# A sequence's mean row put into all rows by one matmul, in a cross-attention and quantised feed-forward kernel

## The chip, the cores and the metric

The kernel runs on one core of one Trainium2 chip. The metric is the device time of one execution in microseconds (us). Each time is the median of the runs named beside it.

## The reference

The reference does one layer on x of shape (4, 2048, 512): four sequences of 2048 rows. First comes cross-attention to a context of 154 rows for each sequence, with 16 heads of 64, and then a feed-forward part with quantised weights.

```
mask = j_idx % n_q == i_idx              # n_q = 2048 rows, n_kv = 154 keys
sim  = where(mask, q @ k^T * scale, -max)
out  = softmax(sim) @ v                  # then @ Wout + bout
x    = x + attention(layernorm(x), context)

h    = layernorm(layernorm(x)) * gamma + beta
h    = qlinear(h, w1, b1)                # rows rounded to 127 steps, w to -1, 0, 1
h    = gelu(h)
x    = x + qlinear(h, w2, b2)
```

The mask leaves query i only key i where i is below 154. For every later row the whole line of scores has one value, so the softmax is even and the row gets the mean of all 154 values. With W = Wv Wout, what attention adds is `context[i] @ W + bout` for rows 0 to 153, and `mean(context) @ W + bout` for rows 154 to 2047. Queries and keys need no arithmetic.

## The kernel before

A tile is 128 rows. There are 64 tiles, 16 for each sequence, and in each sequence the order is tiles 2 to 15, then 0 and 1. So tiles 0 to 13 in the order of work are rows of the first sequence that need only the mean row; tiles 14 and 15 need the 128 first rows ("front") and a mixed tile of 26 keyed rows and 102 mean rows ("second").

Each engine has one queue, in which it works in order. The order of all instructions is written out by hand as strings of words: BEGINNING (line 83) for the start up to tile 11, STEADY (line 118) for four tiles at a time, and ENDING (line 127). A word is a letter code with numbers, and the table `words` maps it to a function. Words of different engines in one string are put into different queues. The words that matter here:

- `lv`, `lo`: load pieces 0 to 7 of Wv and Wout; `w`: four float32 matmuls that add one piece's product into W (line 415); `cw`: copy a quarter of W from PSUM into w_sb (lines 426, 428), on DVE with a last figure of 1 and on ACT with 0.
- `lc`: load the context; `sk`: sum of the keys (line 431); `mk`: mean into row 32b of ctx_rest (434); `lk`: keys 128 to 153 into the rows behind it (437). ctx_rest holds, for each of the four sequences, the mean and the 26 last keys in 32 rows.
- `pr0.2`, `pr2.4`: the product of ctx_rest with W, in two halves of two matmuls (line 444); `yr`: bout added, into y_rest (454); `sr`: y_rest stored to DRAM (481), from which `s` and `t` spread rows of it into `second` and `mean` tiles for the sequences.
- `Yb.0.2`, `Yb.2.4`, `y`: the front rows of sequence b, in two halves (444), and bout added (489).
- `lw`, `ms`, `z`, `q`, `c`: load a chunk of w1 (first figure 0) or w2 (1), sum its absolute values, form the scale of all, round, clip to -1..1. `z` puts a sum of all partitions through PE (`z.1`, "pt", line 206). A last figure of 1 is DVE; with 0 it is ACT for `ms` and `q`, and POOL for `c`.
- `L`: load two tiles of x; `a` (POOL) or `A` (DVE): add the attention row to tile n (246); `S`: row statistics (253); `O`, `o`, `C` or `N`: the scale of the double layer norm for a group of tiles, by DVE with one step on POOL, or all on POOL (269 to 276); `P`, `E` (DVE), or `k` (POOL) or `n` (ACT) with `e` (POOL, lines 311 and 312): normalise and apply gamma and beta; `R`: the largest value of a row (334); `V` (POOL) or `v` (DVE): the group's scales (348, 350); `Q`: round to the 16-bit form (354); `T`: transpose by DMA (365).
- `U`: the up product, 16 matmuls (534); `I`: seed of a half of its PSUM tile with the bias, on ACT or DVE (526, 524); `G`: gelu of a half (553); `M`: its largest value (565); `H`: round (594); `h`: transpose by DMA (605); `W`: the down product, 16 matmuls (612); `D`: its scale (587); `X`, `x`: b2 added (328); `F`, `f`: finish (618) and store.

Groups of tiles for the scales are of sizes 1, 1, 1, 1, 2, 2, 2, 3, 3, and then 4. Group 8 is thus tiles 13 to 15, and `V13` forms the scales of that group. PSUM tiles: three of 1024 columns for `U` (pool ps_h), and two of 512 columns (ps_o), which `pr`, the mean, `z`, `Y` and `W` share. Twelve buffers of one ring hold x pairs and weight chunks; a load waits until a buffer's earlier content has been used.

The mean row of the first sequence is needed first of all. Before, it has a product of its own: `sf` spreads the key sum over 128 columns (line 461), so that `pm` (four matmuls, line 444) writes the mean row of the product into all 128 rows of PSUM. `m` (661) adds bout on DVE and keeps it in SBUF for POOL's additions. For tile 0 `xo` adds bout to x early (476), and `A0` adds the bare product from PSUM.

Of the kernel before, what the change touches and what calls it, by code (L numbers as in the profile page):

```python
# [37 lines left out]
F32 = mybir.dt.float32  # L38
# [3 lines left out]
ALU = mybir.AluOpType  # L42
# [3 lines left out]
P = 128  # L46
# [7 lines left out]
def xattn_ffn(ctx: ExitStack, tc, x, ctxT, WvT, Wout, bout, w1T, b1, w2T, b2, gamma, beta, out):  # L54
    nc = tc.nc
    B, S, D = x.shape
    NKV = ctxT.shape[1] // B
    INNER = Wout.shape[0]
    HID = w1T.shape[1]
    KD, KI, KH = D // P, INNER // P, HID // P  # L60
# [16 lines left out]
    for g, size in enumerate(sizes):  # L77
# [40 lines left out]
    STEADY = """
        U0 G0.0 I1.0.1 M0.0 W-2 G0.1 I1.1.0 M0.1 Q2 F-2 L14 f-2 D-1
# [42 lines left out]
    ones = constant([P, P], F32, "ones")  # L162
# [15 lines left out]
    def x_of(n):  # L178
        return pairs[n // 2][:, n % 2, :]
# [217 lines left out]
    sums = constant([P, KD, B], F32, "sums")  # L397
# [6 lines left out]
    for half in range(2):  # L404
# [4 lines left out]
            start=True,  # L409
            stop=True,  # L410
# [31 lines left out]
    def rows(lhs, dst, ks=range(KD)):  # L442
        for k in ks:
            nc.tensor.matmul(dst, lhs(k), w_sb[k], start=(k == 0), stop=(k == KD - 1))
# [13 lines left out]
    def spread_keys():  # L460
# [170 lines left out]
    def by_half(f):  # L631
# [29 lines left out]
        "m": lambda: nc.vector.tensor_tensor(mean[0], py["mean"], bout_b, ALU.add),  # L661
# [93 lines left out]
```

## Time and profile before

| | |
|---|---|
| median of 3 runs | 524.63 us (524.53 to 524.99) |
| the profiled execution's own time | 525.17 us |
| its span | 523.2 us |
| busy: PE, DVE, ACT, POOL | 501.1, 433.2, 426.3, 410.5 us |
| granted TensorE clock, mean | 0.99 |
| moved by DMA | 94.00 MB, 180 GB/s on average |

The span goes from the first to the last instruction; the execution's own time has 1.97 us around it. Times in the views are microseconds from the start of the span. PE is the matmuls (TensorE), DVE VectorE, ACT ScalarE, POOL GpSimd, SP the engine that issues all DMAs. A line of a timeline gives start, duration, engine, source line, operation, output and inputs, their sizes, the number of instructions merged, and in brackets the idle time before and what ended it. A float32 matmul is two entries there. The granted clock is a share of full speed.

### The profile page before, as it was taken

The page shows a single profiled execution, that of the slowest core. Times are in us where ns is not written, and L with a number is a line of the kernel's source. Part 1 is how long each engine was busy: PE and PEld are TensorE (multiplying, and loading weights), DVE is VectorE, ACT ScalarE, POOL GpSimd, SP SyncE. Part 2 cuts the span into 40 slices and gives each one's busy share as a digit, 9 for nine tenths or more (in the row PEclk, how much of TensorE's full clock was granted, in tenths as well). Part 3 has the DMA queues.
Part 4 walks back from the last instruction along what each step waited for, and adds up shares of the span by engine and source line. Part 5 has one row for each costly group of instructions (what it writes and reads, how often), then busy time and mean ns, then how long its engine had stood idle before and what let it go on. Part 6 is the DMA issues. An engine that isn't in the chain of part 4 may idle for free.

```text
span 523.2 us, 6893 instructions
## 1 busy us (share of the span) xinstructions
PE 501.1 (96%) x2168; PEld 223.8 (43%) x2168; DVE 433.2 (83%) x753; ACT 426.3 (81%) x393; POOL 410.5 (78%) x532
## 2 busy tenths in 40 slices
PE   8997987999999989999999989999999899999996
PEld 3443432444444434444444434444444344444442
DVE  0188999889799889899999988999999888787762
ACT  2278987999788879888888878888889798888971
POOL 0048999999999999899999898999999998852220
PEclk9997998999999999999999999999999999999999
DMA  8998569376979695858697987679586956575664
GB/s 289 399 391 306 188 132 200 84 178 137 195 161 221 141 199 139 201 137 201 149 205 160 178 183 180 164 164 198 133 203 128 201 112 147 110 166 132 135 112 125
DMA packets 194112, 94.00 MB, mean 180 GB/s; under 512 B 170268, under 2 KB 170268, under 8 KB 194076
## 3 DMA queue, kind: packets, MB, share of 16 engines
q1 hardware_dynamic: 194076, 93.56, 75.1%
q8 instruction: 17, 0.28, 0.2%
q14 instruction: 19, 0.16, 0.1%
HBM read 34.55 MB, written 17.04 MB: 99 GB/s over the span
## 4 chain that ended last, share of the span: by engine, by line
PE 57%; POOL 18%; DMA 10%; DVE 6%; ACT 4%; issue 3%; SPq 1%; DVEq 0%; ACTq 0%; POOLq 0%
PE ph L534 27%; PE po L612 26%; DMA xqT<-xqg 6%; PE wps L415 4%; POOL x L246 4%; POOL h L312 3%; POOL h L311 3%; DVE m L565 2%; POOL x L328 2%; DMA x<-x_dram 2%; ACT hq L594 2%; DMA wv<-WvT_dram 2%; POOL h L306 1%; POOL r L270 1%; ACT hid L553 1%
## 5 line engine op out<-in xcount | busy, mean ns | idle before, releaser
L534 PE MATMUL ph<-w1q,xqT 128*128 128x512 f16 x1024 | 233.4, 381 | 10.1 <-DMA xqT<-xqg 7.8
L612 PE MATMUL po<-w2q,hqT 128*128 128x512 f16 x1024 | 231.3, 379 | 1.9 <-DMA hqT<-hq 1.2
L565 DVE TENSOR_REDUCE m<-hid 128x1 f32<-128x1024 f32 (+1 forms) x130 | 153.1, 1192 | 27.0 <-ACT hid L553 26.6
L553 ACT ACTIVATE hid<-ph,d 128x1024 f32<-128x1024 f32 (+1 forms) x130 | 140.9, 1095 | 31.4 <-PE ph L534 30.1
L534 PEld LDWEIGHTS <-xqT 128*128 128x128 f16 x1024 | 100.0, 98 | 135.2 <-DMA xqT<-xqg 12.1
L612 PEld LDWEIGHTS <-hqT 128*128 128x128 f16 x1024 | 100.0, 98 | 123.4 <-DMA hqT<-hq 2.2
L594 ACT ACTIVATE hq<-hid,i 128x2048 f16<-128x2048 f32 (+1 forms) x65 | 128.2, 1974 | 28.3 <-ACT ph L526 10.2
L526 ACT ACTIVATE ph<-b_b,inv 128x1024 f32<-128x1024 f32 x86 | 95.3, 1112 | 3.2 <-POOL inv L348 2.1
L312 POOL TENSOR_TENSOR h<-h,beta_b 128x512 f32<-128x512 f32 x59 | 75.6, 1282 | 4.6
L311 POOL TENSOR_TENSOR h<-h,gamma_b 128x512 f32<-128x512 f32 x59 | 75.0, 1271 | 3.9
L328 POOL TENSOR_TENSOR x<-x,b_b 128x512 f32<-128x512 f32 x61 | 77.0, 1272 | 0.0
L246 POOL TENSOR_TENSOR x<-x,mean 128x512 f32<-128x512 f32 x52 | 65.7, 1273 | 5.0 <-DVE mean L661 3.8
L618 DVE SCALAR_TENSOR_TENSOR o<-po,d,x 128x512 f32<-128x512 f32 x64 | 47.8, 746 | 16.0 <-PE po L612 10.6
L524 DVE TENSOR_SCALAR ph<-b_b,inv 128x1024 f32<-128x1024 f32 x42 | 53.2, 1267 | 0.6 <-ACT hid L553 0.6
L334 DVE TENSOR_REDUCE m<-h 128x1 f32<-128x512 f32 x64 | 42.9, 673 | 5.0 <-POOL h L312 5.0
L354 ACT ACTIVATE xqg<-h,s 128x512 f16<-128x512 f32 x64 | 45.4, 712 | 1.6 <-DVE s L342 1.6
L587 POOL TENSOR_TENSOR d<-mh,wm 128x1 f32<-128x1 f32 x64 | 12.5, 206 | 41.2 <-DVE mh L580 37.4
L253 DVE BATCH_NORM_STATS2 bn<-x 128x6 f32<-128x512 f32 x64 | 43.4, 679 | 0.6 <-POOL x L246 0.6
L306 POOL TENSOR_SCALAR h<-x,rstd,shift 128x512 f32<-128x512 f32 x54 | 41.9, 776 | 0.2
L415 PE MATMUL wps<-wo,wv 128*128 128x512 f32 x64 | 28.1, 595 | 1.5 <-DMA wv<-WvT_dram 1.5
L222 POOL TENSOR_SCALAR w1q<-wi 128x1024 f16<-128x1024 int16 x6 | 6.3, 1070 | 27.7 <-DVE wi L217 27.5
L415 PEld LDWEIGHTS wps<-wo,wv 128*128 128x128 f32 x64 | 11.9, 190 | 17.3 <-issue 13.9
(76 smaller groups left out, 261.3 us busy)
## 6 DMA issues: line engine op xcount, KB each, us to landing
x<-x_dram SPq DMA_DIRECT2D x32, 512.0 KB, 4.2
out_dram<-o SPq DMA_DIRECT2D x64, 256.0 KB, 2.8
ws<-w1T_dram SPq DMA_DIRECT2D x8, 512.0 KB, 7.2
ws<-w2T_dram SPq DMA_DIRECT2D x8, 512.0 KB, 9.6
wv<-WvT_dram SPq DMA_DIRECT2D x8, 256.0 KB, 8.5
wo<-Wout_dram SPq DMA_DIRECT2D x8, 256.0 KB, 4.5
ctx_sb<-ctxT_dram SPq DMA_DIRECT2D x1, 1232.0 KB
hqT<-hq SPq DMA_TRANSPOSE x65, 4.3
```

The costliest lines, as they stand in the source:

```text
L246: e.tensor_tensor(x_of(n), x_of(n), y, ALU.add)
L311: nc.gpsimd.tensor_tensor(normed[n], normed[n], gamma_b, ALU.mult)
L312: nc.gpsimd.tensor_tensor(normed[n], normed[n], beta_b, ALU.add)
L328: e.tensor_tensor(x_of(n), x_of(n), b2_b, ALU.add)
L415: nc.tensor.matmul(wps[k // 2][:, (k % 2) * 512 : (k % 2 + 1) * 512], wv[c][:, k * P : (k + 1) * P], wo[c], start=(c == 0), stop=(c == KI ...
L524: nc.vector.tensor_scalar(ph, row, d, None, ALU.mult)
L526: nc.scalar.activation(ph, row, AF.Identity, bias=0.0, scale=d)
L534: nc.tensor.matmul(bank[i], xqT[n][:, k, :], w1q[:, k, i * 512 : (i + 1) * 512], start=False, stop=(k == KD - 1), skip_group_check=True,)
L553: nc.scalar.activation(hidden[n][:, i * w : (i + 1) * w], up_ps[n][half][:, lo : lo + w], AF.Gelu, bias=0.0, scale=deq1[g][:, j : j + 1],)
L565: nc.vector.tensor_reduce(m2[:, i : i + 1], hidden[n][:, i * w : (i + 1) * w], AX.X, ALU.max, apply_absolute_value=True,)
L594: nc.scalar.activation(hq[n][:, lo : lo + w], hidden[n][:, lo : lo + w], AF.Identity, bias=0.0, scale=inv2[n],)
L612: nc.tensor.matmul(po, hqT[n][:, k, :], w2q[:, k, :], start=(k == 0), stop=(k == KH - 1))
```

## The change

The mean is no longer a product of its own. Row 0 of y_rest, which is the first sequence's mean row with bout already added, is multiplied by a row of 128 ones: one float32 matmul with a single row on both sides (`pm`), which puts it into all 128 rows of PSUM. `A0` adds that to tile 0, with no `xo` before it. `m0` copies it to SBUF on ACT. So `sf`, `xo` and three matmuls are gone, and both halves of `pr` and `yr` now stand before the mean.

BEGINNING is laid out anew, with nearly the same words in another order: other orders of the loads, seven of eight w1 chunks measured on DVE (three before), one w2 chunk measured on DVE, `lr2` (beta) before five w2 loads, `Y1` and `Y2` before `Y0` and `Y3`, `sr` before U0, and the work of some tiles moved between engines: three more `k` and one more `a` on POOL, one `V` fewer there, three `n` fewer on ACT, and single `c` and `X` words exchanged between POOL and DVE. STEADY and ENDING stay.

```
     BEGINNING = """
...
-        w7 lw1.3 ms1.4.0 sk0 c0.4.0 lw1.7 c0.7.0 cw0.1 q0.1.0 sf c0.0.0 cw1.0 lw1.1 pm0.2
-        lr2 cw3.1 cw2.0 lk q0.3.0 c0.1.1 mk pm2.4 xo1 ms1.6.0 L2 q0.6.1 c0.6.1 L3 ms1.2.0
-        Y0.0.2 m lb0 A0 a1 ms1.5.0 S0 Y0.2.4 ms1.0.0 O0 P0 o0 a2 ms1.3.0 C0 pr0.2 S1
-        ms1.7.0 a3 O1 y0 ms1.1.0 c0.3.0 S2 o1 E0 a5 z1.0 R0 z1.1 z1.2 Q0 O2 Y3.0.2 P1 o2
-        q1.6.0 T0 a6 C2 q1.2.0 L4 C1 lb1 V0 lr3 q1.0.0 E1 c1.2.0 Y3.2.4 R1 I0.0.0 P2 V1
-        q1.3.0 pr2.4 a4 y3 S3 Q1 a8 I0.1.0 T1
-        U0 O3 S4 L5 L6 c1.6.0 q1.7.0 S5 o3 E2 end G0.0 c1.0.0 C3 I1.0.0 R2 a7 I1.1.0
...
+        lo0 lv0 lv1 lv2 lw0.5 lo1 lv3 lo2 lv4 w0 lw0.0 lw0.2 lo3 lw0.4 lw0.1 w1 lw0.6 lo4
...
+        sk1 w7 L1 c0.2.0 q0.1.0 sk2 c0.0.0 mk lw1.2 lk cw0.0 cw1.0 c0.6.1 lw1.1 q0.7.0
+        pr0.2 cw3.1 cw2.1 ms1.0.0 c0.7.0 L2 lb0 ms1.6.1 pr2.4 q0.3.0 ms1.3.0 c0.3.0 L3 yr
+        lr3 c0.1.0 pm Y1.0.2 A0 m0 S0 ms1.4.0 a1 O0 P0 ms1.5.0 o0 a2 S1 ms1.2.0 C0 a3
+        ms1.7.0 S2 O1 ms1.1.0 E0 o1 a4 R0 O2 Q0 V0 z1.0 S4 z1.1 a5 I0.0.0 T0 z1.2 lb1 C1
+        sr Y2.0.2 q1.4.0 a6 S5 q1.5.0 L4 o2 P1 N4 q1.1.0 L5 P2 E1 I0.1.0
+        U0 L6 c1.4.1 R1 a7 q1.0.0 C2 Q1 a8 S3 q1.2.0 T1 Y2.2.4 V1 O3 A9 o3 I1.0.0 k5 S6
+        end G0.0 c1.0.0 S7 I1.1.0
+        U1 c1.5.0 y2 C3 k4 G0.1 N6 E2 q1.6.0 P3 Y1.2.4 E3 G1.0 R2 c1.2.0 q1.7.0 Y0.0.2 k7
+        M0.0 Q2 V2 c1.1.0 y1 q1.3.0 T2 Y0.2.4 R3 e4 G1.1 v3 Y3.0.2 M0.1 Q3 I2.0.0 T3 X1 L7
+        t1 I2.1.0 M1.0
+        U2 k6 H0 e5 S8 M1.1 I3.0.0 h0 Y3.2.4 e6 S9 G2.0 R4 G2.1 R5 N8 I3.1.0
+        U3 c1.7.1 A10 Q4 c1.6.1 H1 c1.3.1 T4 D0 y0 L8 V4 M2.0 a13 W0 I4.0.0 h1 y3 X0 L9
+        M2.1 Q5 e7 G3.0 T5 s0 L10 I4.1.0
...
+        U5 a12 G4.1 R8 D1 S13 a11 Q6 M4.1 H3 T6 k9 t2 W2 V6 f0 e9 S11 I6.0.0 h3 F1 G5.0
...
+        U11 T12 M10.0 I12.0.0 M10.1 k16 G11.0 k17 D8 W9 R15 e16 H10 F8 M11.0 G11.1 h10 e17
+        S22 I12.1.0 M11.1 n18 Q13 a23 T13 R16 H11 f8 D10 F9 V13 e18 R17 f9 h11 X11 X10
...
-    first_mean = att.tile([P, KD, P], F32, tag="first_mean", name="first_mean")
-    def spread_keys():
-        nc.vector.tensor_scalar(
-            first_mean, sums[:, :, 0:1].to_broadcast([P, KD, P]), 1.0 / NKV, None, ALU.mult,
-        )
-    def mean_rows(lo, hi):
-        if lo == 0:
-            py["mean"] = ps_o.tile([P, 512], F32, tag="po", name="py_mean")
-        rows(lambda k: first_mean[:, k, :], py["mean"], range(lo, hi))
-    def add_bout(vector):
-        e = nc.vector if vector else nc.gpsimd
-        e.tensor_tensor(x_of(0), x_of(0), bout_b, ALU.add)
+    def mean_rows():
+        py["mean"] = ps_o.tile([P, 512], F32, tag="po", name="py_mean")
+        nc.tensor.matmul(py["mean"], ones[0:1, :], y_rest[0:1, :], start=True, stop=True)
+    def keep_mean(vector):
+        if vector:
+            nc.vector.tensor_copy(mean[0], py["mean"])
+        else:
+            nc.scalar.copy(mean[0], py["mean"])
...
-        "m": lambda: nc.vector.tensor_tensor(mean[0], py["mean"], bout_b, ALU.add),
-        "sf": spread_keys,
-        "xo": add_bout,
+        "m": keep_mean,
```

## The prediction

> **What bounds the kernel now.** I read first how busy each engine is, over the span and by stage.
>
> ```profile
> PE 501.1 (96%) x2168; PEld 223.8 (43%) x2168; DVE 433.2 (83%) x753; ACT 426.3 (81%) x393; POOL 410.5 (78%) x532
> ```
>
> The same by stages:
>
> ```profile
> 40.00:50.00 10.00, 6.32 (x12) 2.76 (x11) 7.91 (x26) 7.50 (x12) 8.71 (x11) 0.75 0.83 301
> 50.00:60.00 10.00, 9.47 (x32) 3.87 (x31) 8.91 (x22) 8.88 (x10) 9.54 (x13) 0.91 0.76 249
> 60.00:70.00 10.00, 10.00 (x36) 4.53 (x35) 9.72 (x19) 9.17 (x11) 9.32 (x16) 1.00 0.33 93
> 70.00:80.00 10.00, 7.47 (x31) 2.97 (x29) 9.76 (x18) 8.70 (x9) 9.26 (x16) 1.00 0.84 192
> 80.00:90.00 10.00, 6.94 (x24) 2.56 (x23) 9.72 (x18) 7.45 (x8) 9.52 (x11) 0.83 1.05 194
> 200.00:480.00 280.00, 276.60 (x1280) 124.90 (x1279) 252.49 (x422) 241.43 (x211) 246.55 (x302) 1.00 0.75 163
> ```
>
> The columns after a stage's length are the busy time of PE, its weight loads, DVE, ACT and POOL, then the granted clock. From 200 to 480 us PE idles 3.4 us of 280: PE sets the pace there. Between 40 and 90 it does not: PE has holes and loses clock, and POOL and DVE are the full ones.
>
> The timeline of PE shows where the holes end (idle in brackets):
>
> ```profile
> 33.76 3.60 PE L444 MATMUL py_mean<-w_sb,first_mean 128*128 128x512 f32 x8
> ...
> 40.62 1.88 PE L444 MATMUL py_rest<-w_sb,ctx_rest 128*128 128x512 f32 x4
> 45.67 0.59 PE L206 MATMUL pt<-tot,ones 128*128 128x1 f32 x2 [3.17 <-DVE tot L203]
> 46.77 6.23 PE L444 MATMUL py<-w_sb,ctx_sb 128*128 128x512 f32 x8 [0.50 <-DVE wm L209]
> ...
> 85.72 5.31 PE L534 MATMUL ph<-w1q,xqT 128*128 128x512 f16 x16 [2.39 <-DMA xqT<-xqg]
> ...
> 190.10 3.63 PE L534 MATMUL ph<-w1q,xqT 128*128 128x512 f16 x16 [2.06 <-DMA xqT<-xqg]
> ```
>
> The line at 85.72 is U4. After it PE runs without a hole until 190.1. So any time won before U4 counts in full only if the other engines can feed U5 to U19 earlier as well. POOL's timeline answers that:
>
> ```profile
> 38.16 1.27 POOL L246 TENSOR_TENSOR x<-x,mean 128x512 f32<-128x512 f32 x1 [3.76 <-DVE mean L661]
> 46.19 1.27 POOL L246 TENSOR_TENSOR x<-x,mean 128x512 f32<-128x512 f32 x1 [1.29 <-DMA x<-x_dram]
> ...
> 150.36 0.19 POOL L348 TENSOR_TENSOR inv<-s,sw 128x3 f32<-128x3 f32 x1
> ```
>
> From a1 (38.16) to V13 (150.36), POOL's gaps over 0.13 us are three: 0.52, 1.29 and 0.29, 2.1 us in 112. POOL is a second bound, running beside PE, from the moment the mean exists. V13 gives the scale of the seed I13.0, which U13 needs, and the margin is small: DVE starts I13.0 at 151.04 (it was waiting for e17 by way of R17; V13's result was there 0.4 us before), ends it at 152.3, and PE takes U13 at 153.03. So U13 could have come 0.7 + 0.4 = 1.1 us earlier as far as V13 goes.
>
> **The change part by part.**
>
> *PE work removed.* A float32 matmul of 512 columns is two passes here: py_mean's four take 3.60 us, 0.9 each. Four go (3.6), one comes. It has one row of weights and data; no row of the trace has such a shape. Below: nothing; above: the two passes of a full one, by py_rest (four passes 1.88, start to start 0.43, the last 0.59), 0.43 + 0.59 = 1.02. The Trainium skill, "TensorE: Matmul & The Clock Gate", section "Why this matters for your kernels", speaks against a cheap row: a single matmul of few rows takes as long as one of 128. By its rule the mean comes 1.0 us after y_rest, in proportion to the rows at once; I take 1.0. Net on PE: 3.6 - 0.9 = 2.7 us less.
>
> *When the mean exists.* Loads: until lo1, 1.83 MB are asked for; before, the third w1 piece, with as much before it, was read at 9.30. So w1 waits about 1.45 us, as w2 did before (1.47), and the 32 products end at 33.9 again. The other seven pieces of Wout and Wv fall in before need at the 0.398 MB/us that the landings at 12.83 (3.15 MB) and 29.15 (9.65 MB) give. DVE: sk, mk, lk are over at about 32.8; cw3, cw2 follow the products, 33.95 to 35.3, inside pr. Then pr, four matmuls, 33.9 to 37.5; yr on DVE 0.68, to 38.2; pm 38.3 to 39.3; ACT copies the mean (by the w_sb copies, 0.59) to 39.95. So a1 starts at 40.0, not 38.16: **1.85 us later**, in spite of less PE work, because y_rest and a trip DVE to PE to ACT lie in the chain. A0 reads PSUM at 39.35, before at 38.00.
>
> *Removed from DVE:* sf 0.67, xo 0.68 and m 0.69, 2.0 us, before A0. DVE gets four more chunks of w1 to measure (seven for three, 1.22 each), at 14 to 26 us under the loads: tot comes at 26.6 after 25.3, and pt sits between w5 and w6, where PE is until 26.9, so nothing is lost; uncovered it would be 1.3 us. ACT sheds as many.
>
> *Until U0.* beta landed at 44.80 and held E0 for 0.73. It is now ordered before five chunks of w2 and lands near 36.5. But the mean is later and tot now stands before S4 on DVE; S1, C0, S2, O1, E0, R0 run from 41.75 to 46.2. ACT has seven measures queued before Q0, the last landing at 44.6, so Q0 starts at 47.0 (46.69 before). T0 goes at 47.65 (47.44). PE has nothing between Y1.0.2 (42.1) and pt (47.2): a hole of 5 us where it was 3.17.
>
> *The clock.* The same page, section "What's actually happening", puts the fall to half clock after an idle window of about 3.4 us. By that rule the old hole (3.17) would cost nothing and the new one would. The rows differ: after 3.17 the clock was 0.50 and Y3 took 6.23, not 3.6; after 2.39, U4 took 5.31, not 3.6; after 2.06 nothing was lost. I go by the rows: both holes cost, so the new one costs no more than the old: Y2.0.2, started at 48.5 behind wm, takes four slow passes, 4.9 us, and U0 starts at 53.4 (54.55 before). By the rule it would be 2.6 us worse against before.
>
> *U0 to U4.* R1 is at 53.85 (51.67) because c1.4, P2, E1 and two stats stand before it, so T1 lands near 60 and U1 is late (58.70 before). Then PE runs U1, Y1.2.4, Y0, Y3.0.2, U2, Y3.2.4, U3, W0: 4 x 3.45 + 10 x 0.9 = 22.8 from 60.3, to 83.1. T4: e5 on POOL ends near 75 to 76, R5, Q4, T4 sent at 78, landed (3.8 by the old one) at 82. U4 at 83.1 with no hole: 2.6 us earlier, and without the 1.7 of lost clock, 4.3 in all.
>
> *SP.* y_rest's store sr now stands before L4, and t1, which reads it back, before h0 (issues of 0.34 and 0.56 by the old rows). The rows are ready by then, and h0 goes out near 72 with W0 due at 79.7, so this is hidden; uncovered it would be 0.9 at W0.
>
> *U5 to U13: what is kept.* POOL's work from a1 to V13, by kind, after minus before: a +1 (1.24), k +3 (0.8 each, 2.4), d +1 (0.15), X -1, c -2 (1.02 each), inv/d pair -1 (0.3): +0.2. Its start +1.85. Its waits: only L2's landing at 46.15 is seen, 0.85 in place of 2.1: -1.25. V13 is thus +0.8 if POOL's slow instructions recur (c at 1.56 and 1.43, h at 1.60 twice against 1.02 and 1.27: about 2 us before V13), and -1.2 if none does. I take the middle, -0.2 to 0, call it **0**. Then U13 comes 1.1 us earlier, not 4.3: PE gives back about 3 in small waits at U6 (V6 at 96 to 97.5 sets I6.0; 94.7 before), at W4 (h4 behind H4 on ACT) and at U13. Behind V13, X11 and X10 move ahead of N20: +1.07 for group 10, for which R19 leads to H14 and I16; U16 had 2.1 us of room, so 1.0 stays. From there on PE has the same work.
>
> *Sum.* Profiled execution: span 523.2, its own time 525.17 (1.97 around it). 523.2 - 1.1 = 522.1, or 524.07 with what lies around; the median of the runs is 0.54 under the profiled one: **523.5**.
>
> **Rivals.**
>
> *The lead survives.* If POOL meets no slow instruction and V13 is over 1 us early, and ACT keeps up, the 4.3 at U4 stay but for small change: 524.6 - 4 = 520.6. For it: U4 was the last hole for 100 us. Against: ACT's and POOL's rows of 80 to 150 are full too.
>
> *Nothing is left.* V13 at +1 and the rooms at U13 and U16 used up: 524.6. For it: the sum of POOL's work is not smaller, and the mean is later.
>
> *Slower, by the clock.* PE reaches U13 4 us ahead, V13 comes at +1 or later, and the hole before U13 passes the length at which the clock falls (between 2.06 and 2.39 by the rows). U13 then takes 5.3, not 3.6: +1.7, with 0.1 from V13: 526.4. For it: two such holes already cost 2.6 and 1.7. Against: waits at U6 and W4 share the lead out in pieces under 2 us.
>
> **How the numbers follow.** My own chain 0.40 (523.5, alone 522.6 to 524.4), the lead survives 0.22, nothing left 0.15, slower by the clock 0.23. 0.2% is 1.05 us, about what a measurement of this kernel can tell from no change. Faster: 0.28 of my chain and 0.22; same: 0.12 and 0.14; slower: 0.23 and 0.01. The range goes from the first rival with one more us (519.5) to the last with 0.4 more (526.8).
>
> **What would show it.** The mean copied near 39.9 and a1 at 40; one py_mean matmul of two passes; U0 near 53.4 behind a slow Y2; U1 near 60; U4 near 83 at full clock; V13 within 1.2 us of 150.4; PE waits at U6 and U13 for seeds. It is wrong if U0 or U1 come much earlier, if POOL's V13 is before 148.5, or if a stall of transposes or a slow U13 shows after 140.

## The result, and the profile after

| | before | after |
|---|---|---|
| median | 524.58 us | 528.38 us (527.17 to 528.67) |
| profiled execution's own time | 525.17 us | 528.67 us |
| its span | 523.2 us | 526.9 us |
| ratio after / before | | 1.0065, 95% interval 1.0049 to 1.0081 |

The changed kernel is slower by 3.8 us between the medians, 3.4 by the ratio, where 1.1 us less was forecast. Measured again in a later batch, the ratio was 1.0067 (1.0050 to 1.0083). First the busy line of the page, of the kernel after:

```profile
PE 499.8 (95%) x2162; PEld 222.1 (42%) x2162; DVE 433.6 (82%) x754; ACT 421.1 (80%) x383; POOL 413.6 (79%) x534
```

PE's work went down and the span went up, so the time is in waits. The stages of the kernel after (columns as in the table of before: length, busy PE, weight loads, DVE, ACT, POOL, then clock, DMA share, GB/s):

```profile
40.00:50.00 10.00, 3.13 (x7) 1.53 (x6) 8.78 (x26) 8.82 (x15) 9.32 (x10) 0.80 0.85 306
50.00:60.00 10.00, 8.04 (x23) 2.68 (x21) 7.14 (x20) 6.17 (x7) 7.21 (x15) 0.86 0.88 248
60.00:70.00 10.00, 8.77 (x29) 4.04 (x30) 9.72 (x19) 8.91 (x10) 9.34 (x18) 1.00 0.08 15
80.00:90.00 10.00, 8.69 (x41) 3.75 (x40) 9.13 (x16) 7.94 (x8) 9.26 (x17) 1.00 0.81 190
200.00:480.00 280.00, 277.46 (x1285) 125.22 (x1284) 253.49 (x424) 242.20 (x212) 247.37 (x304) 1.00 0.75 163
```

Between 50 and 60 POOL is busy for 7.21 of 10 us (8.71 to 9.54 in all stages of before that were shown). That is new. Its timeline, kernel after, names its wait for the mean and the one wait over 0.13 us between a1 and V13 (idle in brackets):

```profile
40.68 1.26 POOL L244 TENSOR_TENSOR x<-x,mean 128x512 f32<-128x512 f32 x1 [2.13 <-ACT mean L463]
...
57.76 1.75 POOL L244 TENSOR_TENSOR x<-x,mean 128x512 f32<-128x512 f32 x1 [2.12 <-DMA x<-x_dram]
...
153.35 0.20 POOL L346 TENSOR_TENSOR inv<-s,sw 128x3 f32<-128x3 f32 x1
```

V13 ends up 3.0 us later than before. PE's timeline, kernel after, shows where that arrives:

```profile
38.13 1.12 PE L457 MATMUL py_mean<-y_rest,ones 1*128 1x512 f32 x2 [0.78 <-DVE y_rest L452]
...
47.21 0.59 PE L204 MATMUL pt<-tot,ones 128*128 128x1 f32 x2 [6.05 <-DVE tot L201]
48.62 3.78 PE L442 MATMUL py<-w_sb,ctx_sb 128*128 128x512 f32 x4 [0.82 <-DVE wm L207]
...
61.23 3.70 PE L521 MATMUL ph<-w1q,xqT 128*128 128x512 f16 x16 [2.78 <-DMA xqT<-xqg]
...
82.80 3.61 PE L599 MATMUL po<-w2q,hqT 128*128 128x512 f16 x16 [1.31 <-DVE front L476]
...
155.02 3.62 PE L521 MATMUL ph<-w1q,xqT 128*128 128x512 f16 x16 [0.57 <-DVE ph L511]
...
193.01 5.20 PE L521 MATMUL ph<-w1q,xqT 128*128 128x512 f16 x16 [2.32 <-DMA xqT<-xqg]
```

U13 starts at 155.02 instead of 153.03 (+2.0). U18 starts at 193.01 instead of 190.10 (+2.9) and takes 5.20 us (3.63 before), because the granted clock is 0.51 in its first 3.3 us. PE is then 4.5 behind. Of this 0.8 comes back at the three later waits for transposes and the last one (0.66, 0.57, 1.30, 0.32 after; 0.45, 1.33, 1.62, 0.29 before), which leaves the 3.7 by which the spans differ.

The way from POOL to U18 is read off DVE's and SP's timelines of the kernel after:

```profile
180.14 0.69 DVE L332 TENSOR_REDUCE m<-h 128x1 f32<-128x512 f32 x1 [0.90 <-POOL h L310]
...
186.27 0.75 DVE L605 SCALAR_TENSOR_TENSOR o<-po,d,x 128x512 f32<-128x512 f32 x1
```

```profile
187.05 0.36 SPq L610 DMA_DIRECT2D out_dram<-o  x1
187.51 1.23 SPq L363 DMA_TRANSPOSE xqT<-xqg  x1
```

and the same three places of the kernel before:

```profile
176.10 0.69 DVE L334 TENSOR_REDUCE m<-h 128x1 f32<-128x512 f32 x1 [0.91 <-POOL h L312]
...
182.23 0.75 DVE L618 SCALAR_TENSOR_TENSOR o<-po,d,x 128x512 f32<-128x512 f32 x1
```

```profile
183.01 0.36 SPq L623 DMA_DIRECT2D out_dram<-o  x1
183.48 1.70 SPq L365 DMA_TRANSPOSE xqT<-xqg  x1
```

R20 on DVE waits for e20 on POOL (the number behind a letter is the tile); behind R20, in DVE's order, stand I17.0, M16 and F14; the store f14 waits for F14; T18 stands behind f14 on SP. From R20's start to T18's issue it is 7.37 us after and 7.38 before. The whole 4.0 us that e20 is late reach T18. From T18's issue to U18 it was 5.50 us after and 6.62 before, so that 2.9 of the 4.0 reach U18. Before, R20 waited for POOL too, with the same 0.9 us: POOL's lag did set T18 already, and the forecast looked for it only as far as V13.

The chain that the profile follows back from the last instruction, to what released each step, runs the same way. Pieces of it in the kernel after (start, length, what):

```profile
50.87 0.51 SPq L468
...
51.47 6.13 DMA x<-x_dram
...
57.76 1.75 POOL x L244
...
178.84 1.28 POOL h L310
...
187.51 5.45 DMA xqT<-xqg
```

It goes over the store `sr` (line 468) and L4 to POOL, and stays on POOL from 57.76 to 180.12, but for 1.2 us on DVE. In the kernel before it is on POOL from 106.1 to 176.08 and goes on to T18 in the same way: POOL was on the chain there too.

### The profile page after: what moved, and what is told of

The parts are those of the page before. It is cut to its first block, busy times and chain, and to the rows that moved or that the text cites. A ratio compares the mean times of both kernels' runs of the same rounds, so it can differ in the third digit from the quotient of the medians.

```text
span 526.9 us, 6889 instructions
## 1 busy us (share of the span) xinstructions
PE 499.8 (95%) x2162; PEld 222.1 (42%) x2162; DVE 433.6 (82%) x754; ACT 421.1 (80%) x383; POOL 413.6 (79%) x534
## 4 chain that ended last, share of the span: by engine, by line
PE 56%; POOL 23%; DMA 8%; DVE 7%; issue 3%; ACT 2%; SPq 0%; POOLq 0%; DVEq 0%; ACTq 0%
PE ph L521 26%; PE po L599 25%; DMA xqT<-xqg 5%; POOL x L244 5%; PE wps L413 5%; POOL h L310 4%; POOL h L309 4%; POOL x L326 3%; POOL h L304 2%; DVE m L552 2%; ACT hq L581 1%; DMA wo<-Wout_dram 1%; DMA x<-x_dram 1%; POOL r L268 1%; DVE bn L251 1%
## 5 line engine op out<-in xcount | busy, mean ns | idle before, releaser
L513 ACT ACTIVATE ph<-b_b,inv 128x1024 f32<-128x1024 f32 x87 | 96.4, 1111 | 6.8 <-POOL inv L346 4.9
L244 POOL TENSOR_TENSOR x<-x,mean 128x512 f32<-128x512 f32 x53 | 67.5, 1280 | 4.3 <-ACT mean L463 2.1
L511 DVE TENSOR_SCALAR ph<-b_b,inv 128x1024 f32<-128x1024 f32 x41 | 51.9, 1266 | 0.4 <-POOL inv L346 0.4
L304 POOL TENSOR_SCALAR h<-x,rstd,shift 128x512 f32<-128x512 f32 x57 | 44.4, 779 | 0.2
L220 POOL TENSOR_SCALAR w1q<-wi 128x1024 f16<-128x1024 int16 x7 | 7.6, 1098 | 29.6 <-DVE wi L215 26.8
L226 DVE TENSOR_REDUCE part<-ws 128x1 f32<-128x1024 f32 x8 | 9.4, 1213 | 17.9 <-DMA ws<-w1T_dram 17.9
```

Of the source, the lines that this page charges most:

```text
L244: e.tensor_tensor(x_of(n), x_of(n), y, ALU.add)
L304: nc.gpsimd.tensor_scalar(h, x_of(n), rstd[g][:, j : j + 1], shift[g][:, j : j + 1], ALU.mult, ALU.add)
L513: nc.scalar.activation(ph, row, AF.Identity, bias=0.0, scale=d)
```

## The experiments

Theory A: POOL's wait for L4, carried by V13 to U13, and further to U18's clock. B: PE's own holes in the front. C: the mean's lateness as such. D: POOL's load and lateness up to V13, of which A and C are parts. E: ACT is as full as POOL, so that work moved to it gains nothing. F, formed last: the time goes by POOL's lag at e20, which sets T18; V13 is only a part of it. A diff is against the changed kernel unless it names another base. Each ratio is to before as measured beside the run on the same chip; e1 to e4, e5 to e8, e9 to e11, e12, e13 to e16, and e17 with e18 were measured together. The expectations call the tiles 9, 12, 13, 14, 15 and 17 of the moved normalisations groups. The landmarks of all runs, each from its own profiled execution:

| run | a1 | V13 | U13 | T18 issued | U18 | ratio to before (95%) |
|---|---|---|---|---|---|---|
| before | 38.16 | 150.36 | 153.03 | 183.48 | 190.10 | 1 |
| changed | 40.68 | 153.35 | 155.02 | 187.51 | 193.01 | 1.0065 (1.0049 to 1.0081) |
| e1 L4 early | 40.93 | 151.50 | 153.15 | 185.68 | 190.20 | 1.0048 (1.0034 to 1.0063) |
| e2 old mean, new layout | 39.04 | 151.19 | 152.86 | 185.41 | 191.24 | 1.0041 (1.0016 to 1.0066) |
| e3 new mean, old layout | 40.23 | 151.46 | 153.56 | 184.58 | 190.18 | 0.9995 (0.9981 to 1.0008) |
| e4 hole of U18 filled | 41.29 | 152.32 | 153.98 | 186.48 | 191.65 | 1.0055 (1.0036 to 1.0075) |
| e5 POOL less | 41.12 | 150.93 | 153.96 | 185.05 | 189.99 | 1.0015 (0.9998 to 1.0033) |
| e6 POOL less, L4 early | 41.28 | 149.53 | 152.84 | 183.68 | 189.83 | 0.9983 (0.9970 to 0.9997) |
| e7 old layout, POOL less | 39.77 | 150.50 | 153.69 | 184.41 | 190.13 | 0.9955 (0.9937 to 0.9974) |
| e8 before, POOL less | 37.60 | 150.08 | 152.47 | 183.17 | 188.26 | 0.9970 (0.9957 to 0.9983) |
| e9 before, POOL more | 38.74 | 153.13 | 155.24 | 186.19 | 191.53 | 1.0032 (1.0021 to 1.0043) |
| e10 as e7, three moved | 39.41 | 149.47 | 153.88 | 183.08 | 188.71 | 0.9959 (0.9947 to 0.9971) |
| e11 as e6, copy first | 39.71 | 149.03 | 152.05 | 183.19 | 188.51 | 0.9978 (0.9968 to 0.9988) |
| e12 as e11, a fourth moved | 40.60 | 150.06 | 153.09 | 184.20 | 189.96 | 0.9992 (0.9981 to 1.0004) |
| e13 L4 early, copy first | 40.13 | 152.01 | 153.68 | 186.24 | 191.28 | 1.0029 (1.0012 to 1.0045) |
| e14 changed, again | 40.59 | 153.76 | 155.42 | 187.91 | 192.83 | 1.0067 (1.0050 to 1.0083) |
| e15 L4 early, again | 40.86 | 151.68 | 153.34 | 185.86 | 190.90 | 1.0029 (1.0012 to 1.0045) |
| e16 new mean, old layout, again | 40.25 | 151.39 | 153.50 | 184.49 | 190.33 | 1.0003 (0.9991 to 1.0015) |
| e17 L4 early, X10 on DVE | 40.44 | 151.44 | 153.10 | 184.38 | 189.31 | 1.0008 (0.9996 to 1.0021) |
| e18 L4 early, X10 ahead of V13 | 40.82 | 152.46 | 154.11 | 185.38 | 190.20 | 1.0026 (1.0015 to 1.0038) |

**L4 early (e1).** Of SP's words around T0 in the kernel after, with the new store of y_rest (line 468) between bias and L4 (line 174, three loads merged):

```profile
49.33 0.56 SPq L385 DMA_DIRECT2D b_b<-b_dram  x1
49.98 1.40 SPq L468 DMA_DIRECT2D rest_dram<-y_rest  x1
51.47 1.60 SPq L174 DMA_DIRECT2D x<-x_dram  x3
```

```
-        sr Y2.0.2 q1.4.0 a6 S5 q1.5.0 L4 o2 P1 N4 q1.1.0 L5 P2 E1 I0.1.0
-        U0 L6 c1.4.1 R1 ...
+        Y2.0.2 q1.4.0 L4 a6 S5 q1.5.0 o2 P1 N4 q1.1.0 L5 P2 E1 I0.1.0
+        U0 L6 sr c1.4.1 R1 ...
```

> The changed kernel with one move on SP's queue: the load L4 is issued ahead of the store of y_rest (sr), which goes behind L6; every other queue keeps its order. Theory A (POOL): POOL's wait of 2.1 us for L4 before a8 (55.64 to 57.76) is carried on to V13, V13 holds U13, and what is lost there lengthens the hole before U18 beyond the length at which the clock falls. Then L4 lands near 56, V13 comes near 151.5 instead of 153.35, U13 near 153.3 instead of 155.02, U18 runs at full clock, and the time is 3 to 3.5 us under the changed kernel's: 525. Theory B (PE): the loss is PE's own, from the hole of 6 us before pt, the slow Y2 and the late U1; none of these is touched, so 528.4 stays, within 0.7.

The wait of 2.12 is gone and V13 is 1.85 earlier, as theory A has it. The time follows less: 1.0048 here and 1.0029 when run again (e15), against 1.0065 and 1.0067, so 0.9 to 2.0 us of the 3.4 to 3.5. A is a part.

**Old mean in the new layout (e2).** `sf`, `pm` in four matmuls, `xo` and the addition of bout are put back; `pr` and `yr` come behind the mean, and `ms1.6.1` goes one line down.

```
-        pr0.2 cw3.1 cw2.1 ms1.0.0 c0.7.0 L2 lb0 ms1.6.1 pr2.4 q0.3.0 ms1.3.0 c0.3.0 L3 yr
-        lr3 c0.1.0 pm Y1.0.2 A0 m0 S0 ...
+        pm0.2 cw3.1 cw2.1 ms1.0.0 c0.7.0 L2 lb0 xo1 pm2.4 q0.3.0 ms1.3.0 c0.3.0 L3
+        lr3 c0.1.0 Y1.0.2 m A0 pr0.2 pr2.4 S0 ...
```

> The changed kernel's layout with the mean as it was before: spread keys, four matmuls, bout added on DVE; y_rest's product follows behind it on PE, in the hole before pt. Theory A (POOL): a1 starts near 38.2 again, but a8 still cannot start before L4 has landed at 57.7, so POOL's wait there grows from 2.1 to over 4 us and V13 stays within 0.5 us of 153.35; the time stays at 528, within 0.8. Theory C (the mean's own lateness): the 2.5 us by which a1 is late are what is lost, so the time falls by 2 to 3.5 us, to 525 to 526.5. Theory B (PE): the hole before pt is partly filled, the four matmuls come back (2.7 us of PE work): between 1 us under and 2.7 us over the changed kernel.

a1 is 1.6 us earlier and V13 2.2, yet the ratio stays at 1.0041: the new layout costs with the old mean as well. So C is a part at most. Theory A had POOL's wait for L4 grow here; in the trace it is gone, because `sr`, at the same place ahead of L4, took SP only 0.38 us. So e2 is a second run without that wait, and stands where e1 does.

**New mean in the old layout (e3).** The BEGINNING of before, with the mean made as in the change.

```
 (base: before)
-        q0.1.0 sf c0.0.0 cw1.0 lw1.1 pm0.2
-        lr2 cw3.1 cw2.0 lk q0.3.0 c0.1.1 mk pm2.4 xo1 ms1.6.0 L2 q0.6.1 c0.6.1 L3 ms1.2.0
-        Y0.0.2 m lb0 A0 a1 ...
+        q0.1.0 mk lk c0.0.0 cw1.0 lw1.1 pr0.2
+        lr2 cw3.1 cw2.0 q0.3.0 c0.1.1 pr2.4 ms1.6.0 L2 q0.6.1 c0.6.1 L3 yr ms1.2.0
+        pm Y0.0.2 A0 m0 lb0 a1 ...
```

> The old layout with the new mean only: sf, xo and the four matmuls out; both halves of pr, yr, pm, A0 and the copy on ACT in their place. All else as before. Theory A (POOL): a1 starts near 40.5, 2.4 us later than 38.16, but POOL's waits of 0.5, 1.3 and 0.3 us behind it take up most of that; V13 comes 0.4 to 1.0 later, inside the 1.1 us of room at U13; 524.6, within 0.8. Theory C (the mean's own lateness): 2 to 3 us over before: 527. If the 2.7 us of PE work taken out count: 522.

No difference: 0.9995, and 1.0003 when run again (e16). a1 is 2.1 late, V13 only 1.1, because L2's landing, for which POOL had waited 1.29, now comes first. The new mean costs nothing where such a wait takes its lateness up. What costs is the layout.

**The hole of U18 filled (e4).** Ten extra matmuls run ahead of U18, into the PSUM tile that W16 overwrites; nothing else changes.

```
+            if word == "U2" and n == 16:
+                fill(16, 10)
```

> The changed kernel with ten matmuls more, of 512 columns (2.2 us), in the hole of 2.32 us that PE has before U18; their product goes into the PSUM tile of W16 and is overwritten. Theory of the clock: the hole of 2.32 us is what halves the clock for U18 (5.20 us instead of 3.6). Filled, U18 takes 3.6 and the time falls by 1.6 us to 526.8, although PE has more to do. If the clock falls for another reason, or the loss is made good later, 528.4 stays.

PE's timeline of this kernel shows them, and U18 at full clock:

```profile
189.49 2.32 PE L599 MATMUL po<-w1q,xqT 128*128 128x512 f16 x10
191.65 3.62 PE L521 MATMUL ph<-w1q,xqT 128*128 128x512 f16 x16
```

The ratio is 1.0055. By the difference of the two ratios the clock at U18 is 0.5 us of the 3.4, and the intervals overlap. In the second trace of the changed kernel (e14) U18 kept its clock (3.63 us after a hole of 1.75), and that execution still took 527.43 us, 2.3 more than before's profiled one. It lost 1.7 at U1 (5.31 us after 3.73 idle), but PE still stood 1.75 before U18 for the transpose of T18, issued at 187.91: what was lost at U1 did not set U18. So most of the loss comes without a slow U18.

**POOL less (e5, e6) and the control (e8).** Three normalisations, 0.8 us each, go from POOL to ACT; e6 has L4 early too. In before (e8) it is two.

```
-        ... T6 k9 t2 ...  G6.1 k12 I7.1.1  ... G11.0 k17 D8 ...
+        ... T6 n9 t2 ...  G6.1 n12 I7.1.1  ... G11.0 n17 D8 ...
 (e8, base: before)
-        U10 S18 H8 k13 F5 k15 M9.0 ...
+        U10 S18 H8 n13 F5 n15 M9.0 ...
```

> The changed kernel, with three normalisations of the front (groups 9, 12 and 17) computed on ScalarE instead of GpSimd; 0.8 us each on GpSimd, so 2.4 us less for it ahead of V13 and nothing else changed. Theory D (the new layout gave GpSimd more work and a later start, and its lag at V13 and at e20 sets U13 and, by way of T18, the hole before U18): V13 near 151 instead of 153.35, U13 near 153, e20 near 176.5 and T18 near 185.2, the hole before U18 under 1 us, and the time down by 2 us or more, to a ratio of 1.002 or less. Theory B (TensorE's own holes and clock in the front): V13 comes earlier, but U13 by less than 0.5 us, and the ratio stays near 1.006. Theory E (ScalarE is as full as GpSimd in this stretch): V13 earlier by under 1 us, because h and F steps on ScalarE come later and GpSimd or TensorE waits for them; ratio 1.005 or more.

> The same three normalisations on ScalarE, and L4 ahead of the store of y_rest on SyncE's queue as well. Theory D: the two gains add: V13 near 149.5, before U13 has need of it; U13 at TensorE's own pace; ratio near 1.000 or below. Theory B: 1.004 as with L4 alone. Theory E: 1.004 to 1.006.

> The kernel before with nothing but the same two normalisations (groups 13 and 15) on ScalarE. It is the control: before has V13 0.4 us ahead of its use and 1.1 us ahead of what U13 needs, so TensorE sets U13 there. Theory D: V13 near 148.8, U13 within 0.4 us of 153.0, ratio 0.999 to 1.001. Theory E: ScalarE late, ratio 1.001 or more. If it is under 0.998, GpSimd held the kernel before as well, at a place that the chain of waits does not show.

D's times hold: 2.4 us less on POOL bring 2.6 us (1.0065 to 1.0015, give or take 1.2 us by the two intervals), and L4 another 1.7, below before. U13 doesn't follow D: it was expected near 153 in e5 and came at 153.96, with no wait for its seed. Theory B falls: e5 keeps the hole of 6.05 us before pt and the slow Y2 behind it (3.77 us). The control was to stay within 0.1% and came to 0.9970, by the reading that its expectation had for such a case: POOL held the kernel before as well. V13 is only 0.28 earlier in its trace (this execution waited 0.9 us more for L2, and 1.13 for ACT's `n13`), and T18 0.31. U18 is 1.84 earlier, since from T18's issue to it there are 5.1 us here and 6.6 in before's trace. So the medians show that two normalisations less on POOL bring 1.6 us; these two traces don't show by which way.

**Old layout, new mean, POOL less (e7); three moved (e10).**

```
 (e7, base: e3)
-        pm Y0.0.2 A0 m0 lb0 a1 ...        U10 S18 H8 k13 F5 k15 M9.0 ...
+        pm Y0.0.2 m0 A0 lb0 a1 ...        U10 S18 H8 n13 F5 n15 M9.0 ...
 (e10, base: e7)
-        ... h8 F6 e13 W7 ...     ... G11.0 k14 e14 W9 ...
+        ... h8 F6 n14 e13 W7 ... ... G11.0 e14 W9 ...
```

> The layout of before with the new mean, ScalarE's copy of the mean put ahead of A0, and two normalisations (groups 13 and 15) on ScalarE instead of GpSimd. Theory D: a1 near 39.7, V13 near 149.3 (151.46 with the new mean alone), U13 where TensorE reaches it, near 152, and the time 1 to 2 us under that of before (ratio 0.996 to 0.998). Theories B and E: ratio 0.999 to 1.001, U13 near 153.5 again.

> The layout of before with the new mean, its copy ahead of A0, and three normalisations (groups 13, 14 and 15) on ScalarE instead of GpSimd; the run with two of them stood at 0.9955. Theory D alone: 0.8 us less again on GpSimd, V13 near 149.7 and ratio 0.994. If TensorE sets the pace by now: 0.9955 as with two. If ScalarE is full (theory E): GpSimd waits over 1 us for it near 130 and H8 and H9 come late, ratio 0.997 or more.

e7 beats both kernels, 0.9955 (0.9937 to 0.9974), some 2.3 us under before; a1 came as expected, V13 1.2 later than expected (0.77 of it a wait for ACT's `n13`). A third normalisation brought V13 another 1.0 earlier and no time (0.9959). DVE's timeline of e10 says why: R20's wait for POOL has shrunk to

```profile
175.15 0.69 DVE L334 TENSOR_REDUCE m<-h 128x1 f32<-128x512 f32 x1 [0.34 <-POOL h L312]
```

and PE reaches U18 with no hole, in both. The chain is then off POOL: from 143.5 to 200 it is PE alone in e10, and in e7 it leaves POOL at 150.5. e7's W0 lost 1.7 us of clock in the front (5.31 us after a hole of 2.21), and e7 is still one of the two fastest: the clock lost there did not show.

Not all of e7's gain is POOL's, as far as the traces show. Its U18 starts where before's does (190.13 and 190.10), so the 2.1 us between the spans lie behind it, in the later waits for transposes (0.42, 0.45, 0.34 and 0.32; before 0.45, 1.33, 1.62 and 0.29). The transpose at 295.8, for one, was issued at the same time in both (295.78 and 295.77), and the up product that waited for it started at 301.86 and 302.73; why the transposes came sooner is open. And e7 stands 0.15% below e8, which has the old mean and also two normalisations less on POOL. The new mean may thus be worth some 0.8 us where POOL has room, but the intervals overlap.

**POOL more, in before (e9).** The counterpart: the three normalisations that the new layout has on POOL, put there in before.

```
 (base: before)
-        ... S10 n9 D2 ...  S16 n12 a17 ...  R15 n17 M11.1 ...
+        ... S10 k9 D2 ...  S16 k12 a17 ...  R15 k17 M11.1 ...
```

> The kernel before, old mean and old layout, with the three normalisations that the new layout gives to GpSimd (groups 9, 12 and 17) moved from ScalarE to GpSimd: 2.4 us more for it ahead of V13, and nothing else. Theory D (what costs time in the change is GpSimd's load up to V13 and e20): V13 near 152.8, U13 near 154.5, T18 near 185.9, the hole before U18 over 3 us and its clock at half, ratio 1.004 to 1.006, as the changed kernel. Theory B (the front's own holes on TensorE) and theory E (ScalarE as full): ratio 0.999 to 1.001.

1.0032 (1.0021 to 1.0043): under what was expected, and half of what the change costs, with V13 as late as in the changed kernel (153.13). U18 kept its clock. So V13 alone doesn't order the kernels: e3 has V13 1.1 late for nothing, e9 2.8 late for half.

**The copy first (e11, e13), a fourth normalisation (e12).** ACT copies the mean before A0 adds it, not after; e13 has this and L4 early alone, e12 has `k14` on ACT too.

```
-        lr3 c0.1.0 pm Y1.0.2 A0 m0 S0 ...
+        lr3 c0.1.0 pm Y1.0.2 m0 A0 S0 ...
 (e12, base: e11)
-        H8 W7 T10 D6 k14 M9.1 ...
+        H8 n14 W7 T10 D6 M9.1 ...
```

> The changed kernel with three normalisations on ScalarE, L4 ahead of the store of y_rest, and ScalarE's copy of the mean ahead of A0; without the last it stood at 0.9983. The copy held a1 by 0.7 us while A0 read the same PSUM tile. Theory D: a1 near 40.5 with the mean at 39.4 or so, V13 0.5 to 0.7 earlier (near 148.9), ratio 0.997 to 0.998. If V13 is no longer what U13 waits for: 0.998 again. If A0's delay counts (it leads to S0 and the first transposes): 0.999 or more.

> The changed kernel with all of the run before (three normalisations on ScalarE, L4 early, the copy of the mean ahead of A0) and a fourth normalisation, group 14, on ScalarE. There U13 stood at TensorE's own pace (152.05), and the one hole left before 270 was U18's, 1.60 us, behind T18 at 183.19. Theory D (group 10's way over GpSimd's e20 sets T18): V13 near 148.2, U13 unmoved near 152, T18 near 182.4, the hole before U18 near 0.8, ratio 0.996 to 0.997. If the transposes set U18 whatever T18's issue: hole 1.6 again and ratio 0.998. Theory E (ScalarE full): W8 or W9 late for hqT, ratio 0.998 or more.

> The changed kernel with L4 ahead of the store of y_rest and ScalarE's copy of the mean ahead of A0; no normalisation is moved. Theory D: V13 near 150.8 (153.35 in the changed kernel, 151.50 with L4 alone), U13 near 152.5, U18 near 190 at full clock; ratio 1.003 if the lag at V13 is what costs, by the slope of about 1 us of time for 1 us of GpSimd that the runs with moved normalisations showed. If what the new layout costs lies elsewhere than in V13's lateness: 1.0045 or more.

e11's a1 wait went from 2.13 to 1.41, and the ratio from 0.9983 to 0.9978, with overlapping intervals. e13 stands at 1.0029, as e15 in the same batch; its V13 was 152.01 and not 150.8, since waits of 0.64 for a weight chunk and 0.48 for x took the copy's 0.7 us. It isn't seen in the time. In e12 POOL waits for ACT, as theory E has it. POOL's timeline of e12:

```profile
130.45 1.27 POOL L309 TENSOR_TENSOR h<-h,gamma_b 128x512 f32<-128x512 f32 x1 [1.46 <-ACT h L297]
```

The 0.8 us taken from POOL came back as a wait of 1.46 for ACT: from a1 to V13 it is 109.5 us, and 109.3 in e11, so the fourth brought POOL nothing. e12 stands above e11, but the intervals touch, and 0.9 of the 1.0 us by which its V13 is later were there at a1, which the edit doesn't touch. That the fourth costs time is not shown.

**The same kernels on one chip (e14, e15, e16).** No edit against the changed kernel, e1 and e3.

> The changed kernel itself, as the base of this batch on the same chip. It stood at 1.0065 with 4 runs. All theories: 1.005 to 1.007, V13 between 152.3 and 153.4, a hole before U18 over 2 us.

> The changed kernel with L4 ahead of the store of y_rest, once more. Before, its profiled execution lost 1.5 us of clock at 415 behind a hole of 2.82. Theory D: V13 151.5, U18 near 190.2, and 1.0045 again if the slow stage at 415 recurs; 1.002 or less if it was one execution's.

> The new mean in the old layout, once more: V13 (151.46) and U18 (190.18) stood as in the run with L4 early, but the time at 0.9995. If V13 and U18 were all that counts, these two would come within 0.1% of each other here; if the layouts differ behind U18 (GpSimd's order of X10, X11 and e18 to e20, or the holes at 302 and 415), this one stays 0.3 to 0.5% lower.

The base held. e15 and e16 have V13 within 0.3 us, U13 within 0.2, and differ by 0.26%: more than V13 and U13 explain, though the intervals overlap by a hair. T18 differs by 1.4 us. In the old layout X10 stands ahead of V13, in the new one behind e18; the same V13 leaves POOL 1.1 us later at e20 (from V13 to R20 it is 26.8 us in e15 and 25.7 in e16). This is theory F.

**X10 moved (e17, e18).** Both have L4 early. e17 gives X10 to DVE at its place; e18 puts it back ahead of V13.

```
 (base: e1)
-        S22 I12.1.0 ... V13 e18 R17 f9 h11 X11 X10
+        S22 I12.1.0 ... V13 e18 R17 f9 h11 X11 x10          (e17)
 (e18: no X10 there, but)
-        U9 ... F5 f4 x6 G9.0 M8.0 W6 ...
+        U9 ... F5 f4 x6 G9.0 X10 M8.0 W6 ...
```

> The changed kernel with L4 early (1.0048 and 1.0029 before), and the addition X10, which the new layout has behind e18 on GpSimd, on VectorE at the same place: GpSimd is 1.27 us lighter between V13 and e20, and V13 itself is untouched (near 151.6). Theory F (the time goes by GpSimd's lag at e20, which sets T18; V13 is only the first part of it): T18 near 184.5 instead of 185.8, as in the new mean on the old layout, and 1.000 to 1.002. Theory D as first put (V13 and U13 set it): 1.003 to 1.0045 again. If VectorE is too full for it: 1.003 or more with T18 as late as before.

> The changed kernel with L4 early, and X10 put back to where the layout of before has it, ahead of V13 on GpSimd: V13 1.27 us later (near 152.9), e20 and T18 as before it (near 185.8). Theory F: the time stays, 1.003 to 1.0045. Theory D as first put: U13 1.2 us later, and 1.005 to 1.007.

Of e17's timeline over the engines, V13 on POOL, R20 on DVE and T18 on SP:

```profile
151.44 0.19 POOL L346 TENSOR_TENSOR inv<-s,sw 128x3 f32<-128x3 f32 x1
...
177.00 0.69 DVE L332 TENSOR_REDUCE m<-h 128x1 f32<-128x512 f32 x1 [0.91 <-POOL h L310]
...
184.38 1.23 SPq L363 DMA_TRANSPOSE xqT<-xqg  x1
```

and the same of e18:

```profile
152.46 0.19 POOL L346 TENSOR_TENSOR inv<-s,sw 128x3 f32<-128x3 f32 x1
...
178.01 0.69 DVE L332 TENSOR_REDUCE m<-h 128x1 f32<-128x512 f32 x1 [0.90 <-POOL h L310]
...
185.38 1.22 SPq L363 DMA_TRANSPOSE xqT<-xqg  x1
```

e17 has V13 where e1 and e15 have it, T18 1.3 to 1.5 earlier, and 1.0008 against 1.0048 and 1.0029. e18 has V13 and U13 0.8 to 1.0 later than those, T18 0.3 to 0.5 earlier, and 1.0026: no slower for the late U13. F is what fits both, D as first put does not. This sets runs of different batches side by side: e17's interval overlaps that of e15, and only e1 lies clear of it. Between e17 and e18, measured together, V13 and T18 differ by 1.0 us alike, so this pair doesn't part the theories. Over the twenty rows of the table the ratio goes with T18's issue (correlation 0.91; with V13 0.85), though each landmark is from one execution and each ratio from many. The line through them rises 0.22%, 1.1 us of time, for each us of T18; it gives the changed kernel 0.67% (0.65 and 0.67 measured) and before -0.21% (0). The odd one out is e7, 0.44% under the line: there R20 did not wait for POOL, so that T18 was not what POOL set, and what e7 gained lies behind U18. So F holds where POOL is on the chain; the rest of the time behind U18 it does not account for.

What isn't settled: how the 3.5 us divide between the lag itself and the clock. Over the executions of e14's batch the mean granted clock was 0.9881 in the changed kernel and 0.9915 in before. Within the changed kernel's executions 0.001 of clock went with 0.26 us, loosely (correlation -0.47), which makes 0.9 us of the difference; but which holes lose clock changes from one execution to the next, and e4 could only remove one of them.

## Why the prediction was wrong

Two steps failed: the store ahead of L4 was put at nothing, and POOL's lag was followed to V13, U13 and U16, but not to U18, where PE had no room.

**"PE work removed": right.** `pm` took 1.12 us where 1.0 was taken. The rule on the matmul of few rows (the Trainium skill, "TensorE: Matmul & The Clock Gate", section "Why this matters for your kernels") held: one row was not cheaper than a full tile's two passes (1.02). The net is 2.5 us less on PE, where 2.7 was summed.

**"When the mean exists": right but for its last link.** The product ended at 39.25 (39.3 forecast). The copy was to run from 39.35, beside A0, which reads the same PSUM tile. It waited for A0, which stands first in the program. ACT's timeline of the kernel after:

```profile
40.01 0.58 ACT L463 COPY mean<-py_mean 128x512 f32<-128x512 f32 x1 [2.55 <-DVE x L244]
```

So a1 came at 40.68 instead of 40.0.

**"SP": the failed step that fed the next.** The store `sr` was said to be hidden. It took 1.40 us of SP (0.34 taken), ahead of L4; L4 landed at about 57.7 and POOL stood for 2.12 us. The prediction named the queue and looked at the rows and at h0, not at L4's own landing. In e2 the store took 0.38 us at the same place, and there was no wait for L4. So the size of the issue looks like the term that failed, though its 1.06 us too much are half of the wait; why it varies is open.

**"U5 to U13: what is kept": the mechanism right, the sum of V13 wrong.** Forecast: start +1.85, composition +0.2, waits -1.25, slow instructions about -0.8, together 0. Measured: start +2.52, waits 2.12 in place of 2.10 (0.0), busy time +0.5, together +3.0. The wait for L2 did go (a4 at 46.32 with no gap), and one for L4 took its place; the slow instructions, whose absence was counted on by half, came again in other places (L4's addition took 1.75, the single-column steps 0.89 against 0.76). From V13 to U13 1.57 was forecast and 1.67 measured, so in this kernel U13 follows V13 as said: it came 2.0 late instead of 1.1 early.

**"X11, X10 ... U16 had 2.1 us of room, so 1.0 stays": wrong, and the costliest.** The room at U16 was looked at, by way of R19. R20, F14, f14 and T18 lead to U18, where PE already stood 2.06 us before: there was no room at all. The sum itself, +1.07 behind V13, was right: from V13 to R20 it is 25.74 before and 26.79 after. It was on that way, on top of V13's 3.0. Behind V13, too, POOL has no wait over 0.3 us up to 212.7 (217.2 after), so nothing takes the lag up. "From there on PE has the same work" is true and of no help. By e17 against e15 and e1 the price of X10 on that way is 0.2 to 0.4%.

**"The clock": half right.** Y2 was to take 4.9 and took 3.78 after a hole of 6.05, at a granted clock of 0.50 throughout. Four passes take 1.88 at full clock and 3.8 at half, so the 4.9 was summed wrong. U0 was 1.2 earlier than forecast. U4 lost nothing, as forecast, but stood at 86.25 and not at 83.1: U1 0.9 later, and 2.1 of waits before W0 (0.80, and 1.31 for PSUM's `front`). U5 was 1.1 ahead of before, U6 0.3. The lead was gone before POOL's lag had its say, so the rival "the lead survives" would have failed at the front too. The rival "slower, by the clock" has the sign, not the place: the hole before U13 was 0.57, the slow stage was U18.

## What to carry to other kernels

When a second engine runs without a gap beside the one that sets the pace, its lag has to be followed past the first place where it shows, through the order of the engines and queues behind it, to every wait where the first engine stands already; that one has no room. Work moved behind the mark that one watches is not free: count it up to the last mark that the engine feeds, and ask where it idles next. Here 2.4 us taken from that engine were worth about 2.6 us of time, until PE had no hole at that place (e10) or ACT made the engine wait (e12). The 2.5 us of matmuls that the change took from TensorE did not show in the time (e3).

## What was not expected of the hardware

The loss of clock does not go by the length of the hole. U18 lost 1.6 us after 2.32 idle in the changed kernel and nothing after 2.66 in e2; U1 nothing to speak of after 2.78 (3.70 us, at a granted clock of 1.00); W0 lost 1.7 after 2.21 in e7; stages at 303 lost 1.4 and 1.7 in e17 and e18 after 2.79 and 2.39:

```profile
302.77 5.06 PE L521 MATMUL ph<-w1q,xqT 128*128 128x512 f16 x16 [2.79 <-DMA xqT<-xqg]
```

(e17's PE timeline.) The Trainium skill, "TensorE: Matmul & The Clock Gate", section "What's actually happening", has a window of about 3.4 us that runs freely, so that it matters where in it a hole lies. That fits rows in which no length parts the holes that lost from those that did not; where the window lay no run here shows. Its 3.4 us of idle window are not what these rows need: by that rule U18 keeps its 3.6 us after 2.32 and W0 after 2.21, and they took 5.20 and 5.31. The prediction's bound "between 2.06 and 2.39" was no bound.

The issue of one and the same store on SP took 1.40 and 1.58 us ahead of L4 (changed, e14), 0.38 at the same place in e2, and 0.42 and 0.60 behind L6 (e1, e15), and from T18's issue to U18 it was 4.5 to 6.6 us, with no order by kernel. The times of the changed kernel's executions lay between 525.1 and 530.7 in e14, those of e16 between 524.7 and 526.3: the new layout is also the less steady one. Why is not shown.
